# Two loads of an adjacency's diagonal made into one, and a load of weights and a verdict moved

## The chip, the cores and the metric

The kernel runs on one core of a Trainium2 chip. The metric is the device time of one execution in microseconds (us); the kernel before took 2150.86 us, the median of three runs (2150.09 to 2152.09).

The engines of the core are called as in the profile: PE (TensorE, matmuls), DVE (VectorE), ACT (ScalarE), POOL (GpSimd) and SP (SyncE). SP and ACT each issue transfers through a queue of their own (q1 for SP, q10 for ACT), and the transfers of both run on the same 16 DMA engines.

## The reference

Two layers over 3327 rows of 512 numbers and one 3327 x 3327 adjacency, all in float32:

```python
h = relu(layernorm(x))
q, k, v = h @ Wq.T + bq, h @ Wk.T + bk, h @ Wv.T + bv
x = x + softmax(q @ k.T / sqrt(512) + adj + adj) @ v

h = relu(layernorm(x))
A2 = adj + eye(N)
dscale = diagonal(A2) ** -0.5
x = x + relu((dscale[:, None] * A2 * dscale[None, :]) @ (A2 @ h @ W.T))
```

The diagonal of the adjacency is needed for one thing only, `dscale`, which scales rows twice: once before the last product and once after it.

## The kernel before

The rows are padded to 26 tiles of 128. The kernel has two stages.

The first stage is the scores. A short start loads the weights, merges `Wq` and `Wk` into one matrix `M`, normalizes the rows of `x` tile by tile, transposes them on PE (`h_transposed`, line 295) and projects them (`project_q`). The start is where all engines depend on each other: SP loads an x tile (`load_x`, line 264), DVE takes its statistics (`norm`, line 182), POOL takes the power, ACT makes the normalized row `ht` (line 302), SP stores this row to `rowd` (line 303), PE transposes it (line 306), and ACT and DVE copy and add the transposed parts to `hp` (lines 309 to 316). The ring for `ht` has four buffers, so a row must be stored before the fourth row after it is made. Then 52 steps (line 785) multiply, take the exponent and store the weights of the attention. They are written with an order that DVE, PE, POOL and SP keep (line 784, `in_order`); ACT is not in that list, so the scheduler of the program is free to place what is issued on ACT. Work for certain steps is put into `at_score` by step number and called at the head of the step (line 786).

The second stage is three large products `g` = 0, 1, 2 with the adjacency or the attention, each in seven products of sub-blocks (`ORDER`, line 30) in two strips, each strip in six steps of two tiles and one step of one. So there are 294 steps, numbered by `number_of(g, product, strip, step)`. A step loads its left operand three steps ahead (line 1319), DVE makes sums of it two steps ahead (line 1357), and PE multiplies (`Step.multiply`, lines 723 and 732). Side work is put at step numbers with `at(k, what)` (line 1210). Work whose name has "load" in it is called at the head of its step; all other work is queued after the step's multiplications and runs among the next step's (lines 1323 and 1373). In this stage `in_order` holds DVE, PE, POOL, ACT and SP (line 1379), so their queues run as the code is written.

The side work around the change, with its steps in the first product:

- `totals` (step 1): the last column sums of the attention weights, which lie in `by_32`, a tile of 128 x 104 with one 32-row block per row of partitions.
- `prepare` (step 2): loads the weights `wvT` in four pieces, the bias `bv` on all partitions, and the diagonal into `dg`, 128 x 26, one column per tile.
- `place_totals` (step 3): DVE makes `tiled`, an identity tiled by 32, in four reductions (line 816); PE multiplies `by_32` with it (line 818); ACT copies the product to `tot` in four copies (line 821).
- `load_diagonal` (step 5): loads the diagonal into `by_32` in the 32-row layout, four times over, one load for each quarter of the partitions (line 889).
- `prepared` (step 6): the reciprocal of `tot`, and `dg` to `sd`, the power -0.5 on POOL (line 899).
- `judge` (step 8): finds on DVE whether all sums are in range, and lets PE add and transpose what it found (lines 848 and 850).
- `judged` (step 9): six operations on DVE that end in the flag `bad`. The flag picks this kernel or the general one at the end.
- `scales` (step 11): `by_32` to the power -0.5, an addition on DVE and a power on POOL (lines 893, 894).

`by_32` is next read in the third product (`Columns.scale`, line 1187). The weights are first used at step `number_of(0, 5, 1, 2)`, in `attend` (line 1065). `post` and `deliver` (lines 930 and 933) put the stores of finished side work on ACT's queue.

Each transfer of SP or ACT takes the next of eight completion semaphores, and its issue waits until the transfer that had this semaphore before it has landed.

Of the kernel before, what the change touches and what calls it, by code (L numbers as in the profile page):

```python
# [10 lines left out]
F32 = mybir.dt.float32  # L11
AF = mybir.ActivationFunctionType
ALU = mybir.AluOpType
AX = mybir.AxisListType

P = 128
# [31 lines left out]
def graph_layers_kernel(  # L48
# [30 lines left out]
    nc = tc.nc  # L79
    NP, D = x.shape  # L80
    DC = D // P
    NT = NP // P
# [12 lines left out]
    def half(k, shape, name):  # L95
        return arena.tile(shape, F32, name=name, tag=f"half{k}")

    def bank(k, name):
        return banks.tile([P, BW], F32, name=name, tag=f"bank{k}")
# [27 lines left out]
    const = ctx.enter_context(tc.tile_pool(name="const", bufs=1))  # L127
# [5 lines left out]
    mhalf = const.tile([P, 1], F32, name="mhalf")  # L133
# [11 lines left out]
    bq_sb = const.tile([P, DC], F32, name="bq_sb")  # L145
    tot = const.tile([P, NT], F32, name="tot")
    by_32 = const.tile([P, NP // 32], F32, name="by_32")

# [273 lines left out]
    ps = [bank(k, "mm") for k in range(DC)]  # L424
    begun = h_transposed(TURN[0], psum_ring(6, 7, 4, 5))
    weighed = half(12, [P, D], "weighed")
    for c in range(DC):
# [5 lines left out]
        else:  # L433
            nc.vector.scalar_tensor_tensor(weighed, w_k[c // 2][:, c % 2], bq_sb[:, c : c + 1], weighed,
                                           op0=ALU.mult, op1=ALU.add)
# [167 lines left out]
    at_score, making = {}, range(44, 52)  # L603
# [143 lines left out]
    steps = [(n, t) for n in range(len(groups)) for t in range(HALF)]  # L747

    def fetch(k):
        if k < len(steps):  # L750
            pairs[k] = Pair(*steps[k])

    def beside_of(k):
        def on(j, what, *args):
            if 0 <= j < len(steps):
                getattr(pairs[j], what)(*args)

        def difference():
            if k < len(steps) and steps[k][1] >= 6:
                next(more_of, None)  # L760

        def open_up(j):
            if (k, j) in opens:
                next(opening)

        return (
            lambda: (on(k - 2, "s4"), on(k - 2, "gather", 0)),
            lambda: (on(k - 1, "s3"), on(k - 2, "gather", 1)),
            lambda: (on(k + 1, "sum_of_adjacency", 0), open_up(2)),
            lambda: (on(k + 1, "sum_of_adjacency", 1), open_up(3)),  # L770
            lambda: (on(k - 2, "total", 0), difference(), open_up(4)),
            lambda: (on(k - 2, "total", 1), on(k - 1, "s1"), next(ahead, None) if k in making else None),
            lambda: (on(k - 1, "s2"), next(ahead, None) if k in making else None),
        )
# [9 lines left out]
    with in_order(*(e.engine for e in (nc.vector, nc.tensor, nc.gpsimd, nc.sync))):  # L784
        for k, (n, t) in enumerate(steps):
            for what in at_score.get(k, ()):
                what()
            if t == 0:
                qt = coming
            fetch(k + 2)  # L790
            if t == 2 and n + 1 < len(groups):
                coming = queries(n + 1)
                more_of = more_queries(n + 1, coming)
            beside = beside_of(k)
            pairs[k].multiply(qt)
        k = len(steps)
        beside = beside_of(k)
        for what in beside[:2]:
            what()
        Chain.finish()  # L800
        for what in (*beside[5:], *beside_of(k + 1)[:2]):
            what()
        for _ in (*ahead, *opening):
            pass
# [5 lines left out]
            y0, y1 = (by_32[:, 4 * (STRIPS[s] + y * HT[s]) : 4 * (STRIPS[s] + (y + 1) * HT[s])] for y in range(2))  # L810
            nc.vector.tensor_sub(y0, y0, y1)

    def place_totals():
        tiled = job_ring([P, P], "tiled")
        for k in range(P // 32):
            nc.vector.tensor_reduce(tiled[:, 32 * k : 32 * k + 32], ident.rearrange("p (a e) -> p e a", e=32), axis=AX.X, op=ALU.add)
        ps = bank(ROLE["p8"], "tot")[:, : 4 * NT]
        nc.tensor.matmul(ps, tiled, by_32, start=True, stop=True)
        ps = ps.rearrange("p (i a) -> p i a", a=4)
        for a in range(4):  # L820
            nc.scalar.copy(tot[32 * a : 32 * a + 32, :], ps[32 * a : 32 * a + 32, :, a])

    steps_of_scores = steps

    ROLE = {"p1": 0, "p6": 2, "p7": 4, "p5": 6, "p2": 7, "p3": 1, "p4": 5, "p8": 3}

    def banks_for(*names):
        return {r: bank(ROLE[r], r) for r in names}  # L830

    verdict = []

    def judge():

        if N < NP:
            other = small.tile([P, 1], F32, name="other")
            nc.vector.tensor_sub(other, tot[:, NT - 2 : NT - 1], tot[:, NT - 1 :])
            nc.vector.scalar_tensor_tensor(tot[:, NT - 1 :], other, padding, tot[:, NT - 1 :], op0=ALU.mult, op1=ALU.add)
        within = small.tile([P, NT], F32, name="within")  # L840
        nc.vector.tensor_scalar(within, tot, SMALL, None, op0=ALU.is_ge)
        good = small.tile([P, NT], F32, name="good")
        nc.vector.scalar_tensor_tensor(good, tot, LARGE, within, op0=ALU.is_le, op1=ALU.mult)
        most = small.tile([P, 2], F32, name="most")
        nc.vector.tensor_reduce(most[:, 0:1], tot, axis=AX.X, op=ALU.max)
        nc.vector.tensor_reduce(most[:, 1:2], tot, axis=AX.X, op=ALU.min)
        ps = bank(ROLE["p8"], "p8")
        nc.tensor.matmul(ps[:1, :NT], ones, good, start=True, stop=True)
        for k in range(2):
            nc.tensor.transpose(ps[:1, (k + 1) * P : (k + 2) * P], most[:, k : k + 1], ident)  # L850
        verdict.append(ps)

    def judged():
        ps, one = verdict[0], small.tile([1, 4], F32, name="one")
# [8 lines left out]
    sd = const.tile([P, NT], F32, name="sd")  # L863
    rs = const.tile([P, NT], F32, name="rs")

    def weights(src):

        w = [half(k, [P, 2, D], "w") for k in (12, 13)]
        for c in range(DC):
            nc.sync.dma_start(w[c // 2][:, c % 2], src[c * P : (c + 1) * P])  # L870
        return [w[c // 2][:, c % 2] for c in range(DC)]

    LD = adjT.shape[1]
    mh = const.tile([P, NT], F32, name="mh")
    nc.vector.memset(mh, -0.5)
    dg = const.tile([P, NT], F32, name="dg")
    bvs = []

    def prepare():
        wv_w1.append(weights(wvT))  # L880
        bvs.append(half(11, [P, D], "bv_sb"))
        nc.sync.dma_start(bvs[0], bass.AP(tensor=bv.tensor, offset=bv.offset, ap=[[0, P], [1, D]]))
        with nc.allow_non_contiguous_dma(reason="the diagonal, once"):
            nc.sync.dma_start(dg, bass.AP(tensor=adjT.tensor, offset=adjT.offset, ap=[[LD + 1, P], [P * (LD + 1), NT]]))

    def load_diagonal():
        with nc.allow_non_contiguous_dma(reason="the diagonal, once"):
            for a in range(4):
                nc.sync.dma_start(by_32[32 * a : 32 * a + 32], bass.AP(tensor=adjT.tensor, offset=adjT.offset,
                                                                      ap=[[LD + 1, 32], [32 * (LD + 1), 4 * NT]]))  # L890

    def scales():
        nc.vector.tensor_scalar(by_32, by_32, 1.0, None, op0=ALU.add)
        nc.gpsimd.tensor_tensor(by_32, by_32, mhalf.to_broadcast(by_32.shape), op=ALU.pow)

    def prepared():
        nc.vector.reciprocal(rs, tot)
# [304 lines left out]
    steps = [Step(g, r, s, t, rights[g, r, t]) for g in range(3) for r in ORDER for s in range(2) for t in every]  # L1202
# [4 lines left out]
    def number_of(g, r, s, t):  # L1207
        return ((g * len(ORDER) + r) * 2 + s) * len(every) + t

    def at(k, what, *args):  # L1210
        between.setdefault(k, []).append((what, args))

    early = []
    for g in range(3):
        for n, r in enumerate(ORDER):
            for t, e in enumerate(every):
                k = number_of(g, n, 0, t)
# [11 lines left out]
    for n, job in enumerate(jobs):  # L1229
        k = k0 + n * (k1 - k0) // len(jobs)  # L1230
# [10 lines left out]
    k = number_of(0, 5, 1, 2)  # L1241
# [6 lines left out]
    k = number_of(1, 5, 1, 2)  # L1248
# [8 lines left out]
    k = number_of(2, 4, 0, 0)  # L1257
# [9 lines left out]
        k += 3 if n < 12 else 2  # L1267
    for n, i in enumerate(range(20, NT, 2)):
        at(number_of(2, 6, 1, 2) + n, last_load, i)
    for k, what in ((1, totals), (3, place_totals), (2, prepare), (6, prepared), (5, load_diagonal), (11, scales), (8, judge), (9, judged)):  # L1270
        at(k, what)
    k = number_of(1, 4, 0, 0)
    at(k, other_weights)
# [491 lines left out]
```

## Time and profile before

| what | value |
|---|---|
| median of three runs | 2150.86 us |
| the profiled execution | 2151.03 us |
| its span, first to last instruction | 2149.1 us |
| PE busy | 2136.7 us, 99% |
| DVE busy | 1653.3 us, 77% |
| ACT busy | 274.0 us, 13% |
| POOL busy | 67.5 us, 3% |
| SP's queue q1 | 374056 packets, 532.72 MB, 75.2% of 16 engines |
| ACT's queue q10 | 28320 packets, 57.95 MB, 7.3% of 16 engines |
| packets under 512 bytes | 139964 of 402498 |

Busy times are of one profiled execution and are shares of its span. A line of the timeline gives start, duration, engine, line of the code, operation, what is written from what is read, and how many instructions were merged into it; in brackets stands how long the engine was idle before, and who ended that. A line of a list of waits gives who waited, for whom, the total in us, how often, and the longest. A line of stretches gives the stretch, its length, the busy time of PE, PE's weight load, DVE, ACT and POOL with the number of instructions, the granted clock of PE, the busy share of the DMA engines and the GB/s that they moved.

### The profile page before, as it was taken

Reading aid. Unit: us, or ns where it says so; the run is one execution under the profiler, and the core shown is the slowest. Engines: PE = TensorE matmul, PEld = TensorE weight load, DVE = VectorE, ACT = ScalarE, POOL = GpSimd, SP = SyncE. Lnnn points to the kernel's source line nnn. Section 1 sums busy time; section 2 is a strip of 40 time slices with the busy share of each in tenths; the row PEclk is TensorE's granted clock in tenths of the full one; section 3 lists DMA queues with packets and bytes.
Section 4 is the critical chain, followed back from the end, with each engine's and each line's share of the span. In section 5 each row is a group of like instructions: output and inputs, shape, how many; then the busy total and the mean of one; then the engine's idle time right before and its main releaser. Section 6 shows DMA issues by size and latency. Waiting matters only on the chain.

```text
span 2149.1 us, 20906 instructions
## 1 busy us (share of the span) xinstructions
PE 2136.7 (99%) x6272; PEld 1181.0 (55%) x6272; DVE 1653.3 (77%) x3235; ACT 274.0 (13%) x441; POOL 67.5 (3%) x63
## 2 busy tenths in 40 slices
PE   9999999999999999999999999999999999999998
PEld 5555555555555555555454555555666665555554
DVE  7479888888897688776777778787466666788888
ACT  5312221112110000001111000000111100000000
POOL 2000000000003000000111000000000000000000
PEclk9999999999999999999999999999999999999999
DMA  8678888888999899888787889986656578978897
GB/s 301 216 255 294 298 308 286 307 291 287 345 309 299 292 369 335 284 301 303 263 306 266 301 281 360 326 313 225 194 158 210 155 210 255 303 224 249 267 284 190
DMA packets 402498, 592.10 MB, mean 276 GB/s; under 512 B 139964, under 2 KB 273480, under 8 KB 402376
## 3 DMA queue, kind: packets, MB, share of 16 engines
q1 hardware_dynamic: 374056, 532.72, 75.2%
q10 hardware_dynamic: 28320, 57.95, 7.3%
q8 instruction: 52, 0.85, 0.2%
q14 instruction: 70, 0.57, 0.1%
HBM read 422.71 MB, written 173.87 MB: 278 GB/s over the span
## 4 chain that ended last, share of the span: by engine, by line
PE 94%; DVE 3%; DMA 1%; issue 1%; POOL 0%; SPq 0%; ACT 0%; DVEq 0%
PE p L732 55%; PE Y L542 13%; PE Z L542 6%; PE p L723 5%; PE p L1056 4%; PE pw L1117 4%; PE X L542 3%; PE Y L398 2%; PE Z L398 1%; PE X L398 0%; DMA wk<-in_wk_dram 0%; DVE part L164 0%; DVE st L185 0%; DMA part<-sum 0%; DMA part<-p 0%
## 5 line engine op out<-in xcount | busy, mean ns | idle before, releaser
L732 PE MATMUL p<-part,b 128*128 128x448 f32 (+1 forms) x3528 | 1257.7, 513 | 0.4 <-ACT p L986 0.2
L732 PEld LDWEIGHTS p<-part,b 128*128 128x128 f32 x3528 | 669.7, 190 | 542.0 <-issue 291.7
L164 DVE TENSOR_TENSOR part<-part 128x896 f32<-128x896 f32 (+1 forms) x252 | 256.7, 1019 | 67.5 <-DMA part<-p 24.2
L542 PE MATMUL Y<-qt,hp 128*128 128x448 f32 (+1 forms) x832 | 308.1, 513 | 0.1
L542 PEld LDWEIGHTS Y<-qt,hp 128*128 128x128 f32 x832 | 157.9, 190 | 133.0 <-issue 73.0
L542 PE MATMUL Z<-qt,hp 128*128 128x384 f32 (+1 forms) x416 | 162.2, 512 | 0.0
L166 DVE TENSOR_TENSOR part<-part,part 128x448 f32<-128x448 f32 (+1 forms) x219 | 129.5, 591 | 15.0
L165 DVE TENSOR_TENSOR part<-part,part 128x448 f32<-128x448 f32 (+1 forms) x219 | 129.4, 591 | 7.3
L723 PE MATMUL p<-part,b 128*128 128x448 f32 (+1 forms) x336 | 124.2, 512 | 0.0
L542 PEld LDWEIGHTS Z<-qt,hp 128*128 128x128 f32 x416 | 79.0, 190 | 66.2 <-issue 37.9
L546 DVE SCALAR_TENSOR_TENSOR g<-g,Y 128x384 f32<-128x384 f32 (+1 forms) x156 | 91.5, 586 | 30.0 <-PE Y L542 28.8
L992 ACT COPY part<-p 128x384 f32<-128x384 f32 (+1 forms) x33 | 16.6, 503 | 656.4 <-PE p L732 466.6
L723 PEld LDWEIGHTS p<-part,b 128*128 128x128 f32 x336 | 63.8, 190 | 54.1 <-issue 31.2
L549 ACT ACTIVATE g<-g 128x768 f32<-128x768 f32 (+1 forms) x48 | 43.1, 898 | 345.7 <-DVE g L546 288.0
L542 PE MATMUL X<-qt,hp 128*128 128x384 f32 (+1 forms) x208 | 81.1, 512 | 0.0
L993 DVE TENSOR_TENSOR part<-p,part 128x384 f32<-128x384 f32 (+1 forms) x33 | 19.3, 585 | 66.0 <-PE p L732 58.4
L1056 PE MATMUL p<-w,ct 128*128 128x512 f32 x136 | 61.6, 592 | 0.0
L542 PEld LDWEIGHTS X<-qt,hp 128*128 128x128 f32 x208 | 39.5, 190 | 33.1 <-issue 19.3
L191 POOL TENSOR_TENSOR rstd<-ve,mhalf 128x1 f32<-128x1 f32 x46 | 38.4, 836 | 528.5 <-DVE ve L189 500.6
L1012 DVE TENSOR_TENSOR ct<-p,part 128x448 f32<-128x448 f32 (+1 forms) x72 | 42.3, 609 | 15.9 <-PE p L723 11.8
L1117 PE MATMUL pw<-w,rows 128*128 128x256 f32 x208 | 53.4, 379 | 0.0
L1047 DVE TENSOR_TENSOR job<-job 128x896 f32<-128x896 f32 (+1 forms) x52 | 52.9, 1018 | 0.0
(194 smaller groups left out, 1680.7 us busy)
## 6 DMA issues: line engine op xcount, KB each, us to landing
part<-sum SPq DMA_DIRECT2D x104, 448.0 KB, 5.0
part<-p SPq DMA_DIRECT2D x91, 448.0 KB, 6.0
part<-sum SPq DMA_DIRECT2D x104, 384.0 KB, 4.2
part<-p SPq DMA_DIRECT2D x91, 384.0 KB, 4.8
part<-in_adjT_dram SPq DMA_DIRECT2D x78, 448.0 KB, 5.0
b<-row SPq DMA_DIRECT2D x234, 128.0 KB, 4.8
part<-in_adjT_dram SPq DMA_DIRECT2D x78, 384.0 KB, 3.8
g<-in_adjT_dram SPq DMA_DIRECT2D x52, 448.0 KB, 4.1
```

Source lines behind the costliest of these rows:

```text
L164: yield nc.vector.tensor_add(o[:, 0:2], g[:, 0:4:3], g[:, 1:2].to_broadcast([P, 2, g.shape[-1]]))
L165: yield nc.vector.tensor_add(o[:, 2], o[:, 1], g[:, 0])
L166: yield nc.vector.tensor_add(o[:, 3], o[:, 2], g[:, 2])
L398: nc.tensor.matmul(ps[:, :w], M[B[name]][:, c, o * P : (o + 1) * P], hp[k][:, A[name], c], start=start and c == 0, stop=c == 1, skip_group ...
L542: nc.tensor.matmul(ps[:, :wd], h_of(self.t, name, k), qt[B[name]][:, k], start=start and k == 0, stop=k == 1, skip_group_check=True)
L546: nc.vector.scalar_tensor_tensor(a[n], a[n], 2.0, ps[:, :wd], op0=ALU.mult, op1=ALU.add if sign > 0 else ALU.subtract)
L549: nc.scalar.activation(g[1], g[1], AF.Exp, **({"bias": pad} if self.t == HALF - 1 else {}))
L723: yield nc.tensor.matmul(ps[("p2", "p3", "p4", "p8")[k]][:, :w], b[:, z], a[:, 0, y], start=k == 3 and not self.seeded, stop=True, skip_gr ...
L732: yield nc.tensor.matmul(ps[r][:, :w], b[:, i], m, start=self.t == 0 and not adds, stop=self.t == PAIRS - 1 and r in ("p1", "p5", "p6", "p ...
L1047: nc.vector.tensor_add(self.a, self.a, self.b)
L1056: nc.tensor.matmul(ps, cts[s][y][d][:, k * P : (k + 1) * P], w[d], start=d == 0, stop=d == DC - 1)
L1117: nc.tensor.matmul(ps, a, W[B[name]][:, c], start=new and c == 0, stop=c == 1, skip_group_check=True)
```

## The change

The diagonal is loaded once, into `dg`, by ACT's queue, from step 20 of the scores. Its second layout in `by_32` is no longer loaded, added to and raised to a power: ACT copies it from `sd` in sixteen small copies (`place_scales`, step 12 of the first product). `prepare`, now only the weights and the bias, goes to step `number_of(0, 4, 1, 1)`, in the fifth of the seven products. The making of `tiled` gets a function of its own, one step ahead of `place_totals`. What PE does for the verdict (`judge_sums`) is put one step after `judge`, and `judged` one step after that.

```diff
+    dg = const.tile([P, NT], F32, name="dg")
...
+    def load_diagonal():
+        step = adjT.shape[1] + 1
+        with nc.allow_non_contiguous_dma(reason="the diagonal, once"):
+            nc.scalar.dma_start(dg, bass.AP(tensor=adjT.tensor, offset=adjT.offset, ap=[[step, P], [P * step, NT]]))
+
+    at_score.setdefault(20, []).append(load_diagonal)
...
-    def place_totals():
+    def tile_identity():
         tiled = job_ring([P, P], "tiled")
         for k in range(P // 32):
             nc.vector.tensor_reduce(tiled[:, 32 * k : 32 * k + 32], ident.rearrange("p (a e) -> p e a", e=32), axis=AX.X, op=ALU.add)
+        verdict.append(tiled)
+
+    def place_totals():
+        tiled = verdict.pop()
         ps = bank(ROLE["p8"], "tot")[:, : 4 * NT]
...
-        ps = bank(ROLE["p8"], "p8")
+        verdict.extend((good, most))
+
+    def judge_sums():
+        ps, (good, most) = bank(ROLE["p8"], "p8"), verdict
         nc.tensor.matmul(ps[:1, :NT], ones, good, start=True, stop=True)
         for k in range(2):
             nc.tensor.transpose(ps[:1, (k + 1) * P : (k + 2) * P], most[:, k : k + 1], ident)
-        verdict.append(ps)
+        verdict[:] = [ps]
...
-        with nc.allow_non_contiguous_dma(reason="the diagonal, once"):
-            nc.sync.dma_start(dg, bass.AP(tensor=adjT.tensor, offset=adjT.offset, ap=[[LD + 1, P], [P * (LD + 1), NT]]))
-
-    def load_diagonal():
-        with nc.allow_non_contiguous_dma(reason="the diagonal, once"):
-            for a in range(4):
-                nc.sync.dma_start(by_32[32 * a : 32 * a + 32], bass.AP(tensor=adjT.tensor, offset=adjT.offset,
-                                                                      ap=[[LD + 1, 32], [32 * (LD + 1), 4 * NT]]))
-
-    def scales():
-        nc.vector.tensor_scalar(by_32, by_32, 1.0, None, op0=ALU.add)
-        nc.gpsimd.tensor_tensor(by_32, by_32, mhalf.to_broadcast(by_32.shape), op=ALU.pow)
+
+    def place_scales():
+        for a in range(4):
+            to = by_32[32 * a : 32 * a + 32].rearrange("p (i b) -> p b i", b=4)
+            for b in range(4):
+                nc.scalar.copy(to[:, b], sd[32 * b : 32 * b + 32])
...
-    for k, what in ((1, totals), (3, place_totals), (2, prepare), (6, prepared), (5, load_diagonal), (11, scales), (8, judge), (9, judged)):
+    for k, what in ((1, totals), (2, tile_identity), (3, place_totals), (6, prepared), (8, judge), (9, judge_sums), (10, judged),
+                    (12, place_scales), (number_of(0, 4, 1, 1), prepare)):
         at(k, what)
```

More of the change, by code (lines that the diff above doesn't have):

```diff
@@ L821, in place_totals @@
             nc.scalar.copy(tot[32 * a : 32 * a + 32, :], ps[32 * a : 32 * a + 32, :, a])
-    steps_of_scores = steps
+    steps_of_scores, verdict = steps, []
     ROLE = {"p1": 0, "p6": 2, "p7": 4, "p5": 6, "p2": 7, "p3": 1, "p4": 5, "p8": 3}
@@ L830, in banks_for @@
         return {r: bank(ROLE[r], r) for r in names}
-    verdict = []
     def judge():
@@ L871, in weights @@
         return [w[c // 2][:, c % 2] for c in range(DC)]
-    LD = adjT.shape[1]
     mh = const.tile([P, NT], F32, name="mh")
     nc.vector.memset(mh, -0.5)
-    dg = const.tile([P, NT], F32, name="dg")
     bvs = []
```

## The prediction

> **What bounds the kernel now.** I read the page first, then who waited for whom on PE, then the places of those waits in the timeline.
>
> ```profile
> span 2149.1 us, 20906 instructions
> ...
> PE 2136.7 (99%) x6272; PEld 1181.0 (55%) x6272; DVE 1653.3 (77%) x3235; ACT 274.0 (13%) x441; POOL 67.5 (3%) x63
> ```
>
> PE is busy for all but 12.4 us. Nothing shorter than that can be gained without less PE work, and the change removes no matmul. The waits of PE (us in total, times, longest):
>
> ```profile
> PE tp L306 <- DVE hp L313: 1.9, 2, 1.6
> PE tp L306 <- ACT hp L309: 1.0, 1, 1.0
> PE p L848 <- DVE most L845: 0.6, 1, 0.6
> PE tp L306 <- DVE nb L195: 0.4, 1, 0.4
> PE tot L818 <- DVE tiled L816: 0.2, 1, 0.2
> ```
>
> Besides these, 1.1 us lie before the first matmul and 6.5 us after the last. Only L848 and L818 belong to the code that is edited; the L306 waits lie in the first 31 us, where DVE is busy 4.97 and 5.00 us of the 5 us from 20 to 25 and 25 to 30. There DVE sets the pace. The timeline around the two edited waits:
>
> ```profile
> 631.92 0.67 SPq L884 DMA_DIRECT2D dg<-in_adjT_dram  x1
> ...
> 641.70 10.89 SPq L889 DMA_DIRECT2D by<-in_adjT_dram  x4
> ...
> 661.73 0.96 DVE L164 TENSOR_TENSOR part<-part 128x768 f32<-128x768 f32 x1 [1.02 <-DMA part<-p]
> ...
> 664.85 0.21 PE L848 MATMUL p<-good,ones 128*1 128x26 f32 x2 [0.59 <-DVE most L845]
> ```
>
> and the stretches there (last figures: DMA share, GB/s):
>
> ```profile
> 646.00:648.00 2.00, 2.00 (x7) 1.03 (x6) 0.98 (x2) 0.21 (x1) 0.00 (x0) 1.00 1.11 61
> 652.00:654.00 2.00, 2.00 (x7) 1.01 (x6) 0.87 (x2) 0.00 (x0) 0.00 (x0) 1.00 0.91 6
> 656.00:658.00 2.00, 2.00 (x8) 1.18 (x7) 1.93 (x4) 0.00 (x0) 0.00 (x0) 1.00 1.00 387
> ```
>
> The four `by_32` loads are 13,312 packets of 4 bytes; for some 9 us the DMA engines are busy and move next to nothing. Yet PE is full throughout: its operands are there already. The stall reaches PE only once, through DVE's late sums and the verdict behind them.
>
> **What the Trainium skill says.** DMA: Bandwidth & Descriptors, Queues, rings and completion order: SP's and ACT's queues are separate rings on the same 16 engines, and an engine takes turns between them packet by packet, typically 9 to 17 descriptors each. The trace is finer: the last 16-byte packets of `bq` (ACT's queue, beside SP's 2 KB ones) start at 6.496, 6.580, 6.666 and 6.752 us: one small packet per 84 ns large one. TensorE: Matmul & The Clock Gate, Part 1: an idle window of about 3.4 us halves PE's clock. No stretch shows it; PE's longest wait is 1.6 us.
>
> **The change, part by part.**
> *Verdict's matmul and transposes one step later*: no PE work less, the wait of 0.59 us goes. *Tile of the identity one step sooner*: its four reductions (1.20 us of DVE) now stand ahead of the sums that start at 637.23; those are for the step that PE begins at about 647, seven us away, so nothing is late, and 0.15 us of wait goes. *The six verdict operations on DVE* (1.1 us) swap places with one step's sums, used two steps on: 0.
> *The 13,312 packets, `by_32`'s add (0.20 us) and GpSimd's power (16.96 us) leave*: they held up SP and DVE, not PE, so beyond the waits above: 0.
> *Sixteen ScalarE copies of 32x26*: L821's four took 0.73 us, so 2.9 us. They follow the copy L992 that ends at 680.1; the next thing that ACT does is a store at 684.97. Hidden; without that cover 2.9 us of a store that a job's buffer waits for.
> *Weights and bias (five loads, 1.25 MB) move* to about 915 us. SP has nothing to issue from 915.2 to 918.0, five issues take 2.0 us by L870's row (four in 2.01), the transfer 3.4 us at 390 GB/s, DMA share there is 0.65, operands are fetched three steps ahead, and first use is at 991 us: 0. Nor did their old place cost PE anything.
> *The `dg` load* is written at step 20 of the scores, but ScalarE is not among the engines whose order is held there, and in the built program it stands as ACT's ninth instruction, between the last early `x` load and the table load:
>
> ```
> ACT  ... wk<-in_wk_dram [waits DMAHW4] ; xt<-in_x_dram [waits DMAHW6] ; dg<-in_adjT_dram [waits DMAHW0] ; table load
> SP   ... g<-in_adjT_dram [waits DMAHW5] ; row_4 [DMAHW6] ; row_11 [DMAHW7] ; row_5 [DMAHW0] ; row_12 ; xt ; xt ; xt
> ```
>
> Transfers take eight completion semaphores in turn, and each issue waits for the transfer eight before. So SP's third store of a normalized row now waits for all of `dg`, and the loads of x tiles 12 to 14 stand behind it. Before:
>
> ```profile
> 8.66 0.33 ACTq L266 DMA_DIRECT2D xt<-in_x_dram  x1
> 9.09 1.28 ACT L302 ACT_TABLE_LOAD   x1 [9.09 <-DMA wk<-in_wk_dram]
> 12.00 1.71 ACT L302 ACTIVATE ht<-xt,nb,rstd 128x512 f32<-128x512 f32 x2 [1.63 <-DVE nb L195]
> ...
> 13.14 3.19 SPq L303 DMA_DIRECT2D row<-ht  x4
> ...
> 16.41 1.52 SPq L266 DMA_DIRECT2D xt<-in_x_dram  x3
> ...
> 21.52 0.69 DVE L185 BATCH_NORM_STATS2 st<-xt 128x6 f32<-128x512 f32 x1
> ```
>
> The third of the four stores went at 15.12. ACT first: `dg` waits for the third `wk` load (landed 10.23), takes 0.35 to 0.67 us, then the table 1.28: at most 12.2, against 12.0; the 0.57 us that ACT idles before 14.28 absorb it.
> Then the landing of `dg`. (1) Its 3,328 packets are 208 per engine, behind ACT's last `x` load, whose packets end at 13.36. (2) Until SP stops at its third store, 5.90 MB are issued (twelve weight and x pieces of 0.262 MB on SP, seven on ACT, `g` with 0.39, two rows of 0.262); 4.06 MB have moved by 13.0, so 1.84 MB remain, 4.7 us at 390 GB/s: to 17.7. (3) One small packet per 86 ns in that time: about 50 of 208. (4) The other 158 run alone at 9 ns each: 1.4 us, to 19.1. (5) Before, `dg`'s bulk was done at 638.2, its last packet at 639.75 and it landed at 640.3: 2 us more, to 21.1.
> SP then issues the two stores and, 0.8 us later, the x loads: 21.9. Such loads landed 2.6 to 6.5 us after issue; with an empty queue I take 2.9: 24.8. DVE takes tile 12 at 21.52 now and works without a pause, so it slips by 3.3 us, and `M`'s differences and PE's transposes at 28.25 behind it; after 31 us PE is full and gives nothing back. The third store also frees a buffer that ScalarE's seventh normalized row (21.58) needs: it lands at about 24, a slip of 2.4 us that lies inside the 3.3.
> Bounds: if the engines pass many small packets per turn, `dg` lands at about 17.5 and tile 12 at 21.2: slip 0. If small packets slow the large ones throughout as from 5 to 6 us, where both queues had work and only 254 GB/s moved, 1.84 MB take 7.2 us: landing 23.6, slip 5.8. The middle is my value since the spacing of `bq`'s packets shows the turn, and the dip lasted one microsecond only.
> Sum against the profiled execution of 2151.03 us (span 2149.1, 1.9 around it): -0.59 - 0.15 + 3.3 = +2.6. The median of the runs is 2150.86: 2153.4.
>
> **Rivals.** *Start unharmed* (0.24): the low bound holds; only -0.74 remains, up to +0.7: about 2150.5. For: x tiles have had slack elsewhere, DVE waited for no x tile. Against: the semaphore in turn is sure. *Slower by over 0.2%* (0.25): the start slips by over 5.04 us, so that +4.3 net is passed. That is decided if `dg` lands after 22.8, or if PE then stands still for over 3.4 us at a stretch, where the clock page makes matmuls take twice as long for some 3 us. Near the upper bound: 2156. Against: PE has 7.0 us of work spread over the 10 us from 20 to 30, which breaks the gap up. *Faster by over 0.2%* (0.05): PE would have to lose 4.3 of its 5.9 us of idling before 2143 us or do its matmuls quicker, for which no row speaks.
>
> **How the numbers follow.** 0.2%, 4.3 us, is about what a measurement of this kernel tells from no change. Forecast 0.46, own range 2152.2 to 2155.0. Same: 0.46 + 0.24 = 0.70; slower 0.25; faster 0.05. The range leaves out the lowest and highest tenth: 2150.2 (slip 0, with the median's 0.7 us of scatter) to 2156.4 (slip 6.2).
>
> **What would show it.** Right: `dg` issued by ACT at about 10.3 and landing 10 to 11 us later; a gap of some 5 us in SP's issues from 15; DVE waiting for an `xt` transfer near 22; no wait of PE at the verdict or the tile; PE's first 50 us about 3 us less busy. Wrong: SP's stores pass at 15 to 17, or `dg` lands within 7 us; PE idle at 680 or 991; the clock below 1.00 before 35 us.

## The result and the profile after

The changed kernel takes 2153.76 us, the median of 17 runs (2151.69 to 2158.18), against 2150.86 us of 17 runs of the kernel before beside it (2148.88 to 2152.82). The ratio is 1.0017, with a 95% interval of 1.0009 to 1.0024: 2 to 5 us slower. The ratio itself is below the 0.2% at which the forecast drew its line, though the interval reaches past it, and the median is 0.4 us from the forecast's 2153.4. The profiled execution was one of the slower ones, 2155.4 us.

The page of the changed kernel, span and engines:

```profile
span 2153.6 us, 20914 instructions
...
PE 2138.6 (99%) x6272; PEld 1181.6 (55%) x6272; DVE 1654.5 (77%) x3234; ACT 277.2 (13%) x457; POOL 51.1 (2%) x62
```

The span is 4.5 us longer: PE is busy 1.9 us more, with the same 6272 instructions, and idle 2.6 us more. POOL has lost 16.4 us, which nobody misses. Where PE waits in the changed kernel (who, for whom, total, times, longest):

```profile
PE tp L307 <- DVE hp L314: 1.9, 2, 1.6
PE tp L307 <- ACT hp L310: 1.8, 1, 1.8
PE tp L307 <- ACT ht L303: 1.7, 2, 0.9
...
PE p L733 <- ACT p L991: 0.9, 1, 0.9
```

The waits at the verdict and at the tile are gone. All waits at `tp` lie in the start. One at 790 us is new there: a wait for the seeds of a strip's last step, values that ACT writes into PE's bank before PE adds to them (line 991). Nothing here names the cause; the waits of SP's queue do:

```profile
SPq L304 <- DMA dg<-in_adjT_dram: 6.1, 1, 6.1
```

No such line exists before. SP stood 6.1 us, once, at a store of a normalized row, until the diagonal had landed. The timeline of the changed kernel around it (start, duration, who; in brackets the idle time before it):

```profile
9.44 0.39 ACTq L757 DMA_DIRECT2D dg<-in_adjT_dram  x1
9.92 1.28 ACT L303 ACT_TABLE_LOAD   x1 [9.92 <-DMA xt<-in_x_dram]
...
13.72 8.14 SPq L304 DMA_DIRECT2D row<-ht  x4
...
21.95 1.40 SPq L267 DMA_DIRECT2D xt<-in_x_dram  x3
...
24.86 0.69 DVE L186 BATCH_NORM_STATS2 st<-xt 128x6 f32<-128x512 f32 x1 [3.12 <-DMA xt<-in_x_dram]
...
27.65 0.69 DVE L186 BATCH_NORM_STATS2 st<-xt 128x6 f32<-128x512 f32 x1 [0.65 <-DMA xt<-in_x_dram]
```

Read from the top: ACT issues `dg` at 9.44; it landed 11.6 us later, at 21.05. SP's four row stores took 3.19 us before and 8.14 now. The loads of x tiles 12 to 14 behind them start at 21.95 and not at 16.41. DVE, which worked on without a pause at 21.52, now stands 3.12 us and takes tile 12 at 24.86; at tile 14 it stands again, and is 4.08 us late. PE's matmul that followed a wait for DVE at 28.25 follows one at 32.34, 4.09 us later (the kernel before, then the changed kernel):

```profile
28.25 1.06 PE L306 MATMUL tp<-ident,ht 128*128 128x128 f32 x8 [1.60 <-DVE hp L313]
```

```profile
32.34 1.07 PE L307 MATMUL tp<-ident,ht 128*128 128x128 f32 x8 [1.59 <-DVE hp L314]
```

PE starts the same number of matmuls in both kernels, so the n-th of one trace can be set against the n-th of the other. The changed kernel's are 4.1 us late from 32 us on. At the tile's matmul they make up 0.43 us and at the verdict's place 0.66, and at 790 us they lose 1.0 again; the last is 4.1 us late.

### The profile page after: what moved, and what is told of

Its sections match the earlier page's. It is cut to its first block, busy times and chain, and to the rows that moved or that the text cites. A ratio compares the mean times of both kernels' runs of the same rounds, so it can differ in the third digit from the quotient of the medians.

```text
span 2153.6 us, 20914 instructions
## 1 busy us (share of the span) xinstructions
PE 2138.6 (99%) x6272; PEld 1181.6 (55%) x6272; DVE 1654.5 (77%) x3234; ACT 277.2 (13%) x457; POOL 51.1 (2%) x62
## 4 chain that ended last, share of the span: by engine, by line
PE 95%; DVE 2%; DMA 2%; issue 0%; ACT 0%; SPq 0%; ACTq 0%; POOL 0%; DVEq 0%
PE p L733 56%; PE Y L543 13%; PE Z L543 7%; PE p L724 5%; PE p L1061 4%; PE pw L1122 4%; PE X L543 3%; PE Y L399 2%; PE Z L399 1%; DMA xt<-in_x_dram 1%; PE X L399 0%; DMA part<-p 0%; DMA row<-ht 0%; DVE part L165 0%; PE tp L307 0%
```

## Experiments

Theory A: the semaphore of `dg` comes round to SP's third row store, and what stands behind that store in SP's queue is late. Theory B: no wait is needed; 3,328 small packets slow the loads on the shared DMA engines. Theory C: the start is not the cause, the cost lies in the middle, where copies and weights were moved. Later a fourth question came up, which part of the change brings the gain.

| kernel | median us (runs) | ratio to before, 95% |
|---|---|---|
| changed kernel | 2153.76 (17) | 1.0017, 1.0009 to 1.0024 |
| dg_on_sp | 2149.93 (13) | 0.9998, 0.9989 to 1.0006 |
| before_dg_early | 2155.32 (7) | 1.0028, 1.0017 to 1.0039 |
| dg_half_early | 2150.45 (21) | 1.0002, 0.9995 to 1.0009 |
| dg_twice_early | 2153.45 (20) | 1.0014, 1.0008 to 1.0021 |
| dg_on_pool | 2152.05 (13) | 1.0004, 0.9996 to 1.0012 |
| dg_after_ht4 | 2154.09 (16) | 1.0018, 1.0010 to 1.0026 |
| sp_verdict_old | 2150.12 (13) | 0.9996, 0.9988 to 1.0005 |
| sp_weights_back | 2149.93 (13) | 0.9997, 0.9989 to 1.0005 |
| sp_copies_late | 2149.88 (13) | 0.9998, 0.9990 to 1.0007 |
| before_verdict_new | 2149.85 (13) | 0.9997, 0.9989 to 1.0005 |

The kernel before, run beside them, had medians of 2150.5 to 2150.9.

### The whole change, with the load out of the start

```diff
-            nc.scalar.dma_start(dg, bass.AP(...))
+            nc.sync.dma_start(dg, bass.AP(...))
```

SP's order is held in the scores, so the load stays where it is written and went at 302.3 us.

> The whole change, with the one load of the diagonal on SP's queue, where its order is held at step 20 of the scores, and so away from the start. Theory A (the load's semaphore comes round to SP's third row store and holds the x loads behind it): third store at about 15, DVE takes tile 12 at 21.5, no clock below 1.00 at 25 to 30, and only the two waits that the change removes are left: 0.7 us under the kernel before, 2150.1. Theory B (the small packets slow the x loads on the shared engines, whatever the semaphore): the same here. Theory C (the cost lies in the middle: the copies, the moved weights, ACT's queue): still about 2.9 us above, 2153.8.

Its timeline:

```profile
13.24 2.80 SPq L304 DMA_DIRECT2D row<-ht  x4
...
16.13 1.73 SPq L267 DMA_DIRECT2D xt<-in_x_dram  x3
...
21.28 0.68 DVE L186 BATCH_NORM_STATS2 st<-xt 128x6 f32<-128x512 f32 x1
```

2149.93 us: the change without its early load is 0.7 us below the kernel before, as A and B said, though the interval also holds no gain. C falls: all that was moved in the middle is still moved. The clock of PE did fall, to a mean of 0.70 from 25 to 30 us, against the expectation; from 34 us on PE's matmuls are all the same no later than in the kernel before.

### The early load alone

```diff
 # the kernel before; dg is not loaded in prepare, but:
+    def load_dg():
+        step = adjT.shape[1] + 1
+        with nc.allow_non_contiguous_dma(reason="the diagonal, once"):
+            nc.scalar.dma_start(dg, bass.AP(tensor=adjT.tensor, offset=adjT.offset, ap=[[step, P], [P * step, NT]]))
+    at_score.setdefault(20, []).append(load_dg)
```

> The kernel before with one part of the change alone: the load of dg on ACT's queue, written at step 20 of the scores; the by_32 loads, the weights and the verdict stay as they were. Theories A and B: the start slips by about 4.1 us as in the changed kernel, tile 12 is taken at 24.9, and nothing is gained: 2155.0, ratio 1.0019. Theory C: within 0.5 us of before.

```profile
SPq L304 <- DMA dg<-in_adjT_dram: 3.7, 1, 3.7
```

It took 2155.32 us, 4.7 over the kernel before, and DVE took tile 12 at 24.99, after 2.76 us of waiting. So this one part is enough for the loss. In this execution `dg` was issued at 10.53 and landed after 8.6 us, at 19.1, sooner than in the changed kernel.

### Half of it, and twice

```diff
+    at_score[20] = [lambda: load_diagonal(nc.scalar, 0, 13), lambda: load_diagonal(nc.sync, 13, NT)]
```

> The changed kernel with half of the diagonal's columns (1,664 packets, 104 for each engine) loaded early on ACT's queue and the other half on SP at step 20 of the scores. Theory A: the early half lands about half as long after 13.4 as the whole did (21.05), at 17.2; x tile 12 lands about 3.9 later, at 21.1, when DVE wants it (21.5): slip 0 to 1, so 2150.1 to 2151.0. Theory B: half of the slip of the whole, about 2, so 2152.

SP waited 2.7 us for `dg`, which landed at 17.1 as expected, and issued the x loads at 18.05. But tile 12 came 5.6 us after `dg` had landed and not 3.9, and DVE took it at 22.69, a slip of 1.2 us. The median, 2150.45, lies in A's range, but its interval, 2149.6 to 2152.6, also holds B's 2152, so this run does not tell the two apart.

```diff
             nc.scalar.dma_start(dg, bass.AP(...))
+            nc.scalar.dma_start(dg2, bass.AP(...))
```

The second load goes into a tile that nothing reads.

> The changed kernel with the load of the diagonal issued twice, one behind the other, early on ACT's queue (the second into a tile that nothing reads). Theory A: the second copy lands about 15 us after 13.4, near 28.6, and holds SP's fourth row store; x tiles 12 to 14 land near 32.5, DVE stands 10 to 11 us, PE's clock falls for some us: 2161 to 2165. Theory B: the DMA engines carry both for twice as long but x loads go on between: slip about 8, 2159, with SP's stores not waiting for dg.

Both expectations failed, B's by 5.5 us and A's by more than 7: 2153.45, no more than with one load. The timeline shows why (ACT's queue):

```profile
9.07 0.39 ACTq L758 DMA_DIRECT2D dg<-in_adjT_dram  x1
10.61 4.26 ACTq L759 DMA_DIRECT2D dg<-in_adjT_dram  x1
```

The second issue held ACT for 4.26 us, so the first normalized row came at 16.26 and not at 11.41 as in the changed kernel. SP's stores started at 17.09 and waited only 2.8 us for `dg`; both loads had landed by about 21.9. This run mixes a late ACT with the wait for `dg`, and decides nothing between A and B; it shows that the landing is not in proportion to the packets.

### The packets without SP's wait

Two kernels let the load of `dg` run beside the start's loads without holding the stores that come before tiles 12 to 14. In the first, GpSimd issues the load, as its first work:

```diff
+    nc.gpsimd.dma_start(dg, bass.AP(...))     # behind the first loads, at 1.27 us
-    at_score.setdefault(20, []).append(load_diagonal)
```

> The changed kernel with the load of the diagonal issued by GpSimd, as its first work after the constants of the start. It then has a queue and a semaphore of its own, and its 3,328 small packets run in the first 15 us beside the weights and x tiles. Theory A (SP's turn behind dg's semaphore is the cause): SP's third row store goes by 16.5, tile 12 is taken at 21.3 to 22.3, no wait of SP for dg: 2150.0 to 2151.0. Theory B (the small packets on the shared engines are the cause, without any wait for them): x tiles land 2 to 4 us late, tile 12 at 23.5 or later: 2152 to 2154.

SP never waits for `dg` here. But from 0 to 10 us only 215 GB/s were moved, against 288 in the kernel before. The whole start is later: SP's stores begin at 15.07, and tile 12 is taken at 22.90, between the two expectations. 2152.05 us is B's lower end, but the interval, 2149.9 to 2153.3, also holds A's range. Nor are these the changed kernel's packets: the trace lists the load as 80 packets of 4 to 256 bytes on a queue of GpSimd's, from 6.9 to 9.8 us, and from 7 to 9 us the engines moved 198 and 91 GB/s where the kernel before moved 391 and 399. So a load of single elements can slow the very first weights and tiles, but this run says little of B, since neither the place nor the packets are the changed kernel's. A second kernel puts the small packets nearer to the right place, on ACT behind its fourth row:

```diff
+            made.append(nc.scalar.activation(ht, xt, AF.Relu, bias=bias(), scale=rstd))
+            if len(made) == 4:
+                d = nc.scalar.dma_start(dg, bass.AP(...))
+                after(d, made[-1])            # keeps it behind that row on ACT
```

> The changed kernel with the load of the diagonal held on ACT's queue behind ACT's fourth normalized row, so at about 16.3 instead of 9.4. In the built program dg's semaphore then comes round to SP's store of row_13 (20.65 in the kernel before), behind the loads of x tiles 12 to 14, while the small packets run beside those very loads. Theory A (the wait of SP's third row store is the cause): SP loads x tiles 12 to 14 from 16.4 as in the kernel before, DVE takes tile 12 at 21.3 to 22.3, and nothing later is short: 2150.0 to 2151.0. Theory B (packets on shared engines): the loads are slowed by as much as in the changed kernel, DVE takes tile 12 at 23.5 or later: 2152 to 2154. A mixture: the row_13 store waits for dg until about 23, which delays later x tiles, 2151 to 2152.

SP's wait, and the timeline:

```profile
SPq L311 <- DMA dg<-in_adjT_dram: 5.3, 1, 5.3
```

```profile
13.88 0.39 ACTq L309 DMA_DIRECT2D dg<-in_adjT_dram  x1
...
15.96 1.69 SPq L267 DMA_DIRECT2D xt<-in_x_dram  x3
...
21.00 0.69 DVE L186 BATCH_NORM_STATS2 st<-xt 128x6 f32<-128x512 f32 x1 [0.68 <-DMA xt<-in_x_dram]
...
24.96 0.33 SPq L311 DMA_DIRECT2D row<-ht  x1
```

And the other waits of its first 40 us:

```profile
ACT ht L305 <- DMA row<-ht: 5.8, 4, 2.8
PE tp L314 <- DVE hp L321: 4.4, 2, 2.6
```

This tells A and B apart. The issue came at 13.88, not at 16.3, but the packets ran from 17 to 24 us, beside the loads of tiles 12 to 14. DVE had tile 12 at 21.00, 5.0 us after its issue and sooner than in the kernel before. In two versions without an early load (sp_verdict_old and sp_weights_back, below) DVE also had to wait for this tile, and it came after 5.4 and 5.9 us: no cost of the packets shows in this load. Then the store of row_13, next in the turn of `dg`'s semaphore, left at 24.96, where the kernel before had it at 20.65. Behind it stood stores whose buffers ACT needs: ACT waited 5.8 us for stored rows, and PE 4.4 us for DVE, where it was 1.9 before. The loss is about the changed kernel's, 2154.09, through another victim. A's mechanism holds; A's number, 2150 to 2151, was wrong, since it took what stands behind row_13 to have time to spare. The mixture had named this store, and its 2151 to 2152 is 2 to 3 us too low.

### The other parts, one at a time

Each is an edit of the version with `dg` on SP, but for the last.

```diff
 # sp_verdict_old
-    (1, totals), (2, tile_identity), (3, place_totals), (6, prepared), (8, judge), (9, judge_sums), (10, judged),
+    (1, totals), (3, place_totals), (6, prepared), (8, judge), (9, judged),     # tile and sums made in place
```

> The version with dg on SP's queue at step 20, and the verdict and the tile of the identity put back where the kernel before had them. The waits of 0.6 us at the verdict and 0.2 us at the tile come back. If nothing gives it back: 0.7 us over the version with dg on SP's queue (2149.93), 2150.7. Rival: PE's wait of 0.5 us at the seeds of the strip's last step near 786 us, which the trace of that version shows and the kernel before does not, is where the gain is paid back; then that wait goes as the verdict's comes, and it is 2150.1.

```profile
PE tot L831 <- DVE tiled L824: 0.2, 1, 0.2
```

The tile's wait came back, the verdict's 0.6 us did not, though the verdict stands where it stood. That looks like the work of the 13,312 small packets, which are gone here. But before_dg_early has them still, with the verdict in its old place, and its trace shows no such wait either (DVE's last number for the verdict, then PE's matmul):

```profile
666.62 0.17 DVE L854 TENSOR_REDUCE most<-tot 128x1 f32<-128x26 f32 x1
```

```profile
667.68 0.21 PE L856 MATMUL p<-good,ones 128*1 128x26 f32 x2
```

DVE was done 0.9 us before PE came to the verdict. Only the one trace of the kernel before has this wait; whether the kernel or that execution makes it stays open. 2150.12 does not tell the two expectations apart.

```diff
 # before_verdict_new: the kernel before with this line (and the functions split as in the change)
-    ((1, totals), (3, place_totals), ..., (8, judge), (9, judged))
+    ((1, totals), (2, tile_identity), (3, place_totals), ..., (8, judge), (9, judge_sums), (10, judged))
```

> The kernel before with only the tile of the identity made a step sooner and the verdict's PE work and DVE work each a step later; the diagonal's loads, by_32's add and power and the weights stay. The forecast's step: the waits of 0.59 and 0.15 us of PE go and nothing takes their place, 0.7 us under the kernel before: 2150.1. Rival: the late sums behind the 13,312 small packets reach PE at another place, and it stays within 0.2 us of before.

Both waits went, a wait of 0.3 us at the seeds near 785 us came, and the median, 2149.85, is 0.7 us under the kernel before, with an interval that also holds no gain. Here too DVE was done at 662.0, 0.8 us before PE reached the verdict's old place, so the later step was not needed in this execution. Matmul by matmul, the tile's earlier step gains 0.42 to 0.43 us on the kernel before in each trace with that edit and nothing in the two without; at the verdict's place every trace gains 0.66 to 0.67 us on it, with the later step or without.

```diff
 # sp_weights_back
-    (12, place_scales), (number_of(0, 4, 1, 1), prepare)
+    (2, prepare), (12, place_scales)
 # sp_copies_late
-    (12, place_scales)
+    (number_of(1, 4, 1, 3), place_scales)
```

> The version with dg on SP's queue, and the weights and bias loaded again at step 2 of the products. If the move of these loads costs and gives nothing, as forecast: 2149.9, PE's waits the same. Rival: the wait of 0.5 us near 786 us comes from SP's loads standing in another order since the move, and goes: 2149.4.

> The version with dg on SP's queue, and the sixteen copies of the second layout put off to the second product (from step 12 of the first). If they are hidden where they were, as forecast: 2149.9, PE's waits the same. Rival: the store behind them on ACT at 685 us is late, the job's buffer comes free late, and that is what reaches PE near 786 us as 0.5 us: then that wait goes, 2149.4.

2149.93 and 2149.88: no cost of weights or copies shows in either place. The wait for the seeds near 786 us stayed with the first (1.1 us) and was absent with the second, which looked like a cause.

### The same kernels once more

> The changed kernel once more, for a second trace. If the landing of dg is fixed by the number of its packets it is 21.05 again, within 0.3, and tile 12 is taken at 24.9. If it hangs on which large packets stand beside it, it moves by a microsecond or two (it was 19.1 in the kernel before with the load early), and tile 12 moves with it. PE's wait at the seeds near 790 us: again 0.5 to 1.1 us if the order of the work makes it.

> The version with dg on SP's queue once more, for a second trace. If its wait of 0.5 us near 786 us and the lower clock from 25 to 30 us belong to the kernel, both are there again; if they belong to one execution, at least one is gone. Tile 12 is taken at 20.9 to 21.6 either way.

The second trace of the changed kernel, 2151.43 us (SP's wait, then the timeline):

```profile
SPq L304 <- DMA dg<-in_adjT_dram: 3.7, 1, 3.7
```

```profile
9.44 0.39 ACTq L757 DMA_DIRECT2D dg<-in_adjT_dram  x1
...
19.16 1.42 SPq L267 DMA_DIRECT2D xt<-in_x_dram  x3
...
23.08 0.69 DVE L186 BATCH_NORM_STATS2 st<-xt 128x6 f32<-128x512 f32 x1 [1.58 <-DMA xt<-in_x_dram]
```

Issued at the same 9.44, `dg` landed after 8.8 us and not 11.6, at 18.2. Tile 12 slipped 1.56 us instead of 3.34, and the span was 2149.6 instead of 2153.6. So the landing differs from execution to execution. The chain of work that ended last (start, duration, what) doesn't pass SP's wait here:

```profile
13.62 6.14 DMA row<-ht
...
26.66 3.84 PE Y L399 x6
30.50 1.31 PE tp L307 x8
```

SP's first row store, which waits for no `dg`, landed after 6.14 us, and ACT's fifth row waited for its buffer until 19.86; then PE, at half its clock, was still multiplying when DVE's `hp` was ready at 29.66. PE's matmuls are 2.1 us late from here on, where DVE is 1.6. Whether small packets slowed that row store is not separated: it took 5.9 to 6.3 us in the three traces with one whole load of `dg` issued before it, and 5.1 to 6.0 in the seven with no load in the start.

There was no wait at the seeds, nor in the second trace of dg_on_sp (2148.98 us): that wait belongs to an execution, not to the copies. What makes it is open; it is at most 1.1 us.

## Why the prediction was right

By its own steps:

- **Verdict and tile, -0.59 and -0.15.** Both waits are gone, and without the early load the change stands 0.7 to 0.8 us under the kernel before in three kernels (2149.93, 2149.93, 2149.88). Each interval is 3.4 us wide or more, so the size rests on the traces. By these the tile's step is worth 0.43 us, more than its wait, and the verdict's wait is in no trace but that of the kernel before, so the later step can't be credited with its end. That the sum of the two fits the medians is luck.
- **Packets, add and power leave: 0.** Nothing in the traces speaks against it.
- **Sixteen copies hidden.** Right; they took 3.9 us, not 2.9 (230 to 237 ns each, where the four copies it was worked out from took 172 to 176), and ended at 686.9 without a wait of PE.
- **Weights moved: 0.** Right: issued from 919.4, the weights landed 6.7 to 7.8 us after their issue and not 3.4, and PE did not wait at their use.
- **The semaphore in turn holds SP's third row store.** Right, and the decisive step: it is in the trace, it comes and goes with the load, and where the turn is shifted the loss moves to another store. In the second trace it holds the store too, for 3.7 us, but another chain ends last.
- **`dg` lands at 21.1.** 21.05 in the first trace, by terms of which several were wrong: that they meet is luck, and the second trace has 18.2. The issue was at 9.44, not 10.3, as ACT did not have to wait for `wk`. Term 3, one small packet for each large one, is wrong for the bulk. Counted from the transfers of the first trace, packets of 4 bytes on ACT's queue and megabytes on SP's, begun in each microsecond:

```
us     12    13    14    15    16    17    18    19    20
small  427   1862  321   178   275   141   43    36    77
MB     0.21  0.09  0.19  0.34  0.33  0.34  0.38  0.32  0.01
```

  Two thirds pass by 14 us, and SP's traffic nearly stops for that microsecond; then a tail drips beside the large packets, in place of terms 4 and 5. The landing follows the tail's end: 20.4 here, 17.5 in the second trace. That is as the Trainium skill has it (DMA: Bandwidth & Descriptors, Why a DMA increments its semaphore by 16 and not by 1): each of up to 16 engines reports for itself, and only when all have is the transfer landed. The forecast had bounds of 17.5 and 23.6 for its own ignorance; both executions of the changed kernel lie within them.
- **Tile 12 lands 2.9 us after its issue, slip 3.3.** 2.91 and 3.34 in the first trace. Tile 14's further 0.7 us was not foreseen, and PE was 4.1 us late; in the second trace it was 2.1. The forecast's 3.3 lies between, and its sum, +2.6, meets the +2.9 of the medians, though neither execution went as forecast: the first took 4.4 us more than the profiled execution before, the second 0.4. The size is in part luck.
- **Rival "slower by over 0.2%", from the clock.** The forecast held that PE's work between 20 and 30 us breaks the gap up and keeps the clock. It did not: no wait of PE in the start exceeds 1.8 us, well below the idle window of about 3.4 us that it took from the Trainium skill (TensorE: Matmul & The Clock Gate, Part 1), and the clock fell to half, for 6.83 us (the stretches of the changed kernel; after DVE, ACT and POOL stands the clock):

```profile
21.11:24.52 3.41, 2.12 (x16) 1.67 (x15) 0.16 (x1) 3.41 (x10) 1.26 (x3) 1.00 0.79 257
24.52:27.94 3.42, 2.14 (x6) 1.58 (x7) 2.42 (x8) 2.79 (x7) 0.83 (x2) 0.50 1.03 368
```

  Six matmuls at line 399 took 4.05 us and not 2.10, which is PE's 1.9 us of longer work. In this trace it cost nothing, for PE waited for DVE after them as long as before, 1.59 us. In the second trace, where DVE was less late, PE did not wait after them and lost about 0.5 us (2.1 less DVE's 1.6). So the rival's mechanism was there; it stayed small because DVE was late as well, not because the clock held.
- **Signs.** The clock below 1.00 before 35 us was named as a sign of being wrong. It came, in the changed kernel and also in dg_on_sp, where the start is unharmed, so it tells nothing of the forecast's main step. The landing of `dg` 10 to 11 us after its issue was named as a sign of being right, and 11.6 and 8.8 both miss it.

## What to carry to other kernels

A transfer's landing is waited for not only by its readers but by whoever's turn its semaphore takes next, and all that stands behind that in the queue; so look up in the built program which instruction that is, before a slow transfer goes anywhere near a busy start. Where the written place was not held in order, the load without inputs went near the front of its queue, though it was written in step 20. A wait of PE that one trace shows may belong to that execution: look for it in a trace that keeps its supposed cause before crediting an edit with its end.

## What the runs showed of the hardware

- Small packets pass in bursts: 1,862 of 4 bytes within one microsecond on 16 engines, while SP's queue moved 0.09 MB and not the 0.36 of the kernel before. After the burst a tail of 36 to 321 per microsecond ran beside large packets in the first trace, and its end lay 2.9 us sooner in the second.
- PE's clock fell without any long wait. The traces record it as 1.00 or 0.50, changing on a grid of 3.41 us; values between, as the 0.70 above, are means. Lay each of the 14 traces on its grid and take the share of each cell in which PE multiplies, without the eight matmuls of `pu` (line 453 of the changed kernel), which are one column wide and took 1.05 us. The ten cells at full clock that were followed by half clock have 0.14 to 0.36 (in the changed kernel 2.12 less 1.05 of 3.41 us, 0.31); the lowest that was followed by full clock has 0.42. This was found in the traces afterwards, with the narrow matmuls left out because it fits only so, and no run tested it.
- One issue of 3,328 elements took ACT 0.39 us, and a second right behind it 4.26 us.
